# Ranking the instructions of two mixture-of-experts layers for the scheduler: routings and combinations at the start of the program, experts' blocks 200 places back, the rest as traced

## The chip, the core and the metric

The kernel runs on one core of a Trainium2 chip. Its engines work beside each other, each through its own list of instructions: TensorE (PE, with its weight loads as PEld), VectorE (DVE), ScalarE (ACT) and GpSimd (POOL); SyncE (SP) issues DMAs and computes nothing. GpSimd issues the indirect DMAs of this kernel. The metric is the device time of one execution in microseconds, the median of several runs.

## The reference, cut to what matters

Four layers work on `x` of 4 batches x 1024 tokens x 128 channels. Each is a "macaron": half a feed-forward block, an attention, the same half feed-forward again. All blocks take `layernorm(x)`, and all are added to `x`.

```python
x = x + 0.5 * _L0_ffn_ref(_layernorm(x, axis=-1), ...)   # mixture of 8 experts, gelu, the best 2 of a token
x = x + _L0_attn_ref(_layernorm(x, axis=-1), ...)        # per token: 16 heads against 16 heads
x = x + 0.5 * _L0_ffn_ref(_layernorm(x, axis=-1), ...)
x = x + 0.5 * _L1_ffn_ref(...)                           # gated feed-forward, silu
x = x + _L1_attn_ref(...)                                # full attention over 1024 tokens, rotary
x = x + 0.5 * _L1_ffn_ref(...)
x = x + 0.5 * _L2_ffn_ref(...)                           # mixture of 8 experts, relu, the best 2
x = x + _L2_attn_ref(...)                                # linear attention with decay
x = x + 0.5 * _L2_ffn_ref(...)
# layer 3: RWKV channel mix, time mix, channel mix
```

A mixture layer takes for each token the two experts with the largest router logits, runs each on it (128 to 512, an activation, back to 128), and adds the two results with softmax weights. Layers 0 and 2 are such layers, and the change concerns these alone.

## The kernel before, in words

`x` stays in SBUF as four tiles `x0` to `x3`, one for each batch, channels on partitions. The program has four stages: layer 0 with the first half feed-forward of layer 1; layer 1's attention (its matmuls ordered by hand); layer 2 with the second half feed-forward of layer 1 before it; layer 3.

In layers 0 and 2 the work is cut into tasks. A task is a Python generator: each `yield` ends a step and says what the step costs. The tasks of a pass n (0 ahead of the attention, 1 behind it) and a group of batches are:

- **route** (name `route{n}{first batch}`, line 284 on): normalised rows of the group go to memory (`rows`, line 307, a DMA on SP); logits; the best two of each token; a slot for each token and expert, so that every expert gets whole blocks of 128 slots; from that the index vectors `source` and `target` and the expert of each block. Most of it is a chain of small VectorE instructions. The last part sums 16 matmuls (a group of one batch) or 32 (two) into `held`, and the index vectors are made from it.
- **experts** (`experts{n}{first batch}`, line 421 on): one step a block, 23 blocks for a group of one batch and 39 for two. A block loads its expert's weights (`e_w`, 578 KB, line 455, a DMA on SP, 4 buffers), gathers 128 rows (`e_xg`, line 457, on POOL), transposes them on PE (line 461), copies (`e_x`, DVE), does four matmuls up, each followed by the activation on ACT (`e_h`, line 468), four matmuls down, an add (`e_y`, DVE, line 441) and a scatter to `res` (line 442, on POOL).
- **combine** (`combine{n}{batch}`, line 474 on): reads both results of each token back (`c_y`, line 487, two DMAs on SP, which wait for the group's scatters), weighs and adds them, transposes, and adds half to `x`.
- **middle** (`middle{batch}`): the layer's attention. In layer 0 it is VectorE's work: for each of 8 tiles of 128 tokens two products of 128x2048 (`prod`, lines 528 and 545), two reductions of them (lines 530 and 547), and small instructions. In layer 2 (lines 879 on) it is a recurrence over 8 tiles with some nine matmuls each.
- **last** (layer 0) and **first** (layer 2): layer 1's half feed-forwards.

The groups are (0), (1), (2, 3) in layer 0's first pass and (0, 1), (2), (3) in its second; in layer 2 (0, 1), (2, 3) in both. So layer 0 has 85 + 85 blocks and layer 2 has 78 + 78. A task starts in the trace when the tasks it names are done: experts after their route, combine after its experts, middle after its combine, route1 after the middles of its group.

`lanes` (line 1188) interleaves the tasks: each lane is a list of tasks in order, has a clock, and the lane with the least clock takes the next step and adds its cost. What comes out is only the order in which the instructions are traced. `macaron` (line 1208) makes the lanes: one of experts, one of combinations, and what `layer0` (line 1233) and `layer2` (line 1255) add (attention, feed-forward, routings).

After that a scheduler puts each engine's instructions in their final order. Each instruction has a rank, the value of a counter that goes up with each traced one; of those that could run next on an engine in its planning, the lowest rank goes first. This order is fixed in the program: an instruction that waits holds all behind it on its engine or queue. Before the change the rank is the place in the trace, so the lanes' interleaving decides.

Of the kernel before, what the change touches and what calls it, by code (L numbers as in the profile page):

```python
# [205 lines left out]
class Macaron:  # L206
# [981 lines left out]
    def lanes(self, *lanes):  # L1188
        lanes = [list(lane) for lane in lanes]
        clock, active, done = [0.0] * len(lanes), [None] * len(lanes), set()  # L1190
        while any(lanes) or any(active):
# [13 lines left out]
            else:  # L1205
                clock[n] += cost

    def macaron(self, name, moe, func, groups, marks, more):


        weights, (side, main), wp = self.packs[name + "m"], (self.side, self.main), self.fp
        plans = {}

        def plan(n, group):
            return plans.setdefault((n, group), {"mark": marks[n, group]})

        def route(n, group, *after, ps=side):
            return f"route{n}{group[0]}", after, lambda: self.route(ps, wp, moe, group, plan(n, group))

        def experts(n, group):  # L1220
            names = (f"route{n}{group[0]}",)
            return f"experts{n}{group[0]}", names, lambda: self.experts(main, wp, weights, func, group, plan(n, group))

        def combine(n, group):
            for b in group:
                yield f"combine{n}{b}", (f"experts{n}{group[0]}",), lambda b=b: self.combine(side, wp, group, b, plan(n, group))

        every = [(n, group) for n in range(2) for group in groups[n]]
        blocks = [experts(*g) for g in every]
        back = [task for g in every for task in combine(*g)]  # L1230
        self.lanes(blocks, back, *more(route))
# [140 lines left out]
```

## Time and profile before

| | us |
|---|---|
| median of 3 runs (3285.68 to 3298.78) | 3293.57 |
| the profiled execution | 3296.3 |
| its span, first to last instruction | 3294.4 |
| layer 0, with the loads ahead of it | 0 to about 942 |
| layer 1's attention | about 942 to 2037 |
| layer 2 | about 2037 to 2802 |
| layer 3 | about 2802 to 3294 |

| busy | us | share |
|---|---|---|
| PE | 2875.3 | 87% |
| PEld | 1685.8 | 51% |
| DVE | 1826.5 | 55% |
| ACT | 1649.2 | 50% |
| POOL | 807.0 | 24% |

The ends of some tasks in layer 0, from the instructions' times in the trace: experts00 start on PE at 49.4; experts01 end at 235; combine00 reads at 148.9 and middle0 starts at 160.8; experts02 run from 232 to 387; middle1 ends at 427.4; route10 runs from 430 to 515; experts10 from 515 to 670; middle3 ends at 729; experts13 end at 898. In layer 2: experts02 run from 2289 to 2451, the middles of batches 0 and 1 end at 2422, route10 at 2476; experts10 run from 2479 to 2647, the middles of 2 and 3 end at 2593, route12 runs from 2591 to 2650, experts12 from 2653 to 2781.

The page of the profile gives busy time of each engine, the granted clock of TensorE, the chain of work that ended last, and the costliest groups of instructions. A matmul's end is modelled, so a busy PE is not a PE at its peak. Idle time of an engine matters only where the chain goes through it.

### The profile page before, as it was taken

The page shows a single profiled execution, that of the slowest core. Times are in us where ns is not written, and L with a number is a line of the kernel's source. Part 1 is how long each engine was busy: PE and PEld are TensorE (multiplying, and loading weights), DVE is VectorE, ACT ScalarE, POOL GpSimd, SP SyncE. Part 2 cuts the span into 40 slices and gives each one's busy share as a digit, 9 for nine tenths or more (in the row PEclk, how much of TensorE's full clock was granted, in tenths as well). Part 3 has the DMA queues.
Part 4 walks back from the last instruction along what each step waited for, and adds up shares of the span by engine and source line. Part 5 has one row for each costly group of instructions (what it writes and reads, how often), then busy time and mean ns, then how long its engine had stood idle before and what let it go on. Part 6 is the DMA issues. An engine that isn't in the chain of part 4 may idle for free.

```text
span 3294.4 us, 48535 instructions
## 1 busy us (share of the span) xinstructions
PE 2875.3 (87%) x18206; PEld 1685.8 (51%) x18206; DVE 1826.5 (55%) x3160; ACT 1649.2 (50%) x3640; POOL 807.0 (24%) x748
## 2 busy tenths in 40 slices
PE   6888637878879999999999999988988977899997
PEld 6766426766643333333333333586777865344333
DVE  3376877774226676676776772431555521355664
ACT  3565524658613565566566565444444534444442
POOL 2565405552340000000000000046434454011110
PEclk7989858889977999999999999979989988788997
DMA  4766414663500000000000000157565666000000
GB/s 151 227 186 188 140 42 130 185 188 115 168 9 7 4 6 4 6 6 4 21 5 6 1 1 9 42 152 245 171 185 147 199 197 194 0 0 0 7 7 13
DMA packets 122890, 277.64 MB, mean 84 GB/s; under 512 B 18016, under 2 KB 67296, under 8 KB 122528
## 3 DMA queue, kind: packets, MB, share of 16 engines
q1 hardware_dynamic: 101792, 231.77, 23.8%
q0 software_dynamic: 20864, 42.77, 4.3%
q8 instruction: 144, 2.36, 0.3%
q14 instruction: 90, 0.74, 0.1%
HBM read 238.43 MB, written 31.85 MB: 82 GB/s over the span
## 4 chain that ended last, share of the span: by engine, by line
PE 74%; DVE 12%; ACT 5%; issue 4%; DMA 3%; POOL 1%; another core or an unknown queue 0%; SPq 0%; ACTq 0%; DVEq 0%; POOLq 0%
PE bank L227 40%; PE two L227 17%; PE o L227 8%; PE s L227 4%; DVE nm L720 2%; ACT e_h L468 2%; PE wave L1010 1%; DVE prod L545 1%; PE bank L461 1%; DMA c_y<-res 1%; DVE sc L530 1%; ACT L468 1%; DMA e_w<-in_l0m_dram 1%; DVE prod L528 1%; DVE e_x L463 1%
## 5 line engine op out<-in xcount | busy, mean ns | idle before, releaser
L720 DVE TENSOR_REDUCE nm<-two 128x2 f32<-128x1024 f32 x512 | 626.9, 1225 | 288.3 <-PE s L227 268.9
L743 ACT ACTIVATE e<-s 128x512 f32<-128x512 f32 x1024 | 556.4, 595 | 405.6 <-PE s L227 402.6
L468 ACT ACTIVATE e_h<-bank,e_w 128x128 f32<-128x128 f32 x1304 | 454.8, 368 | 511.6 <-PE bank L227 388.4
L227 PE MATMUL bank<-e_x,e_w 128*128 128x128 f32 x2608 | 569.3, 318 | 154.5 <-ACT e_h L468 79.9
L227 PE MATMUL s<-qm,kz 32*128 32x512 f32 x2048 | 634.1, 643 | 0.8 <-ACT e L743 0.8
L227 PE MATMUL two<-kz,qz 32*128 32x512 f32 x2048 | 593.2, 664 | 21.3 <-DVE nm L720 2.5
L227 PEld LDWEIGHTS bank<-e_x,e_w 128*128 128x128 f32 x2608 | 413.9, 204 | 291.3 <-ACT e_h L468 144.4
L457 POOL DMA_INDIRECT e_xg<-rows,g_source x326 | 334.4, 1026 | 835.1 <-DVE g_target L412 354.2
L227 PE MATMUL bank<-e_w,e_h 128*128 128x128 f32 x2608 | 445.7, 291 | 12.3 <-ACT e_h L468 6.9
L442 POOL DMA_INDIRECT res<-e_y,g_target x326 | 373.5, 1146 | 337.0 <-DVE e_y L441 152.7
L227 PEld LDWEIGHTS bank<-e_w,e_h 128*128 128x128 f32 x2608 | 378.8, 205 | 23.0 <-ACT e_h L468 13.3
L227 PE MATMUL o<-e,va 128*32 128x256 f32 x4096 | 328.8, 392 | 0.1
L441 DVE TENSOR_TENSOR e_y<-bank,e_w 128x128 f32<-128x128 f32 x326 | 94.3, 290 | 403.7 <-PE bank L227 317.0
L227 PEld LDWEIGHTS two<-kz,qz 32*128 32x128 f32 x2048 | 159.7, 189 | 239.9 <-issue 164.0
L227 PEld LDWEIGHTS o<-e,va 128*32 128x32 f32 x4096 | 81.0, 108 | 390.3 <-issue 370.3
L227 PEld LDWEIGHTS s<-qm,kz 32*128 32x128 f32 x2048 | 206.9, 183 | 10.9 <-issue 7.7
L708 POOL COPY va<-vd 128x256 f32<-128x256 f32 x16 | 6.7, 433 | 626.3 <-PE o L227 538.0
L1115 POOL TENSOR_TENSOR z<-st,r 128x512 f32<-128x512 f32 x32 | 46.2, 1445 | 417.1 <-DVE st L1108 333.7
L463 DVE COPY e_x<-bank 128x128 f32<-128x128 f32 x326 | 93.0, 285 | 92.2 <-PE bank L461 67.6
L227 PE MATMUL bank<-g_cols,g_lanes 128*128 128x39 f32 (+1 forms) x512 | 90.5, 341 | 28.9 <-DVE g_cols L392 28.8
L461 PE MATMUL bank<-c,e_xg 128*128 128x128 f32 x326 | 95.0, 291 | 21.7 <-DMA e_xg<-rows,g_source 21.6
L227 PEld LDWEIGHTS bank<-g_cols,g_lanes 128*128 128x128 f32 x512 | 91.2, 270 | 32.5 <-issue 31.4
(300 smaller groups left out, 3694.0 us busy)
## 6 DMA issues: line engine op xcount, KB each, us to landing
e_w<-in_l0m_dram SPq DMA_DIRECT2D x170, 578.0 KB
e_w<-in_l2m_dram SPq DMA_DIRECT2D x156, 578.0 KB
c_y<-res SPq DMA_DIRECT2D x32, 512.0 KB
rows<-g_xt SPq DMA_DIRECT2D x16, 512.0 KB
e_xg<-rows,g_source POOLq DMA_INDIRECT x326
res<-e_y,g_target POOLq DMA_INDIRECT x326
x<-in_x_dram SPq DMA_DIRECT2D x4, 512.0 KB
qz<-qd SPq DMA_DIRECT2D x64, 32.0 KB
```

The lines of the kernel that those rows point to most:

```text
L227: self.nc.tensor.matmul(out, lhsT, rhs, start=start, stop=stop)
L441: nc.vector.tensor_tensor(y, o, w[:, MOE_W - D :], ALU.add)
L442: ins = nc.gpsimd.indirect_dma_start(out=res[:, :], out_offset=at(target[:, k : k + 1]), in_=y, in_offset=None)
L457: nc.gpsimd.indirect_dma_start(out=xg, out_offset=None, in_=rows[:, :], in_offset=at(source[:, k : k + 1]))
L461: nc.tensor.transpose(tp, xg, self.c0["ident"])
L463: nc.vector.tensor_copy(x, tp)
L468: nc.scalar.activation(h[:, fc, :], up[:, fc, :], func, bias=w[:, 2 * FC * P + fc : 2 * FC * P + fc + 1])
L528: v.tensor_tensor(pr, q.unsqueeze(2).to_broadcast(sh), k.unsqueeze(1).to_broadcast(sh), ALU.mult)
L530: v.tensor_reduce(sc, pr, AX.X, ALU.add)
L720: v.tensor_reduce(nm[:, it, h, 2 * pair : 2 * pair + 2], s, AX.X, ALU.max, negate=True)
L743: nc.scalar.activation(es[g], s, AF.Exp, scale=scale)
L1115: (pool if i else v).tensor_tensor(z, st[:, 0:HALF], r, ALU.mult)
```

## The change

A new generator `ahead` runs each step of a task inside the scheduler library's context `high_priority(offset)`. With no offset the counter is set to 0, the start of the program, for the instructions of that step; with an offset it is set back by so much, and can fall below 0. At the end of the step the counter has its old value again, so instructions of such steps do not advance it. Routings and combinations are wrapped without an offset, experts with 200. Attention and feed-forward are not wrapped; they alone advance the counter, by some 130 for a middle of layer 0. What the tasks compute, their tiles and the lanes stay as they are.

```diff
+    def ahead(self, task, offset=None):
+
+        while True:
+            with self.tc.high_priority(offset=offset):
+                cost = next(task, None)
+            if cost is None:
+                return
+            yield cost
...
         def route(n, group, *after, ps=side):
-            return f"route{n}{group[0]}", after, lambda: self.route(ps, wp, moe, group, plan(n, group))
+            return f"route{n}{group[0]}", after, lambda: self.ahead(self.route(ps, wp, moe, group, plan(n, group)))
 
         def experts(n, group):
             names = (f"route{n}{group[0]}",)
-            return f"experts{n}{group[0]}", names, lambda: self.experts(main, wp, weights, func, group, plan(n, group))
+            return f"experts{n}{group[0]}", names, lambda: self.ahead(self.experts(main, wp, weights, func, group, plan(n, group)), 200)
 
         def combine(n, group):
             for b in group:
-                yield f"combine{n}{b}", (f"experts{n}{group[0]}",), lambda b=b: self.combine(side, wp, group, b, plan(n, group))
+                yield f"combine{n}{b}", (f"experts{n}{group[0]}",), lambda b=b: self.ahead(self.combine(side, wp, group, b, plan(n, group)))
```

## The prediction

> **What bounds the kernel now.** I read the chain that ended last first, to see which engine carries the end; then the busy times by stretch, to see where that engine stands idle; then the experts' blocks counted by stretch; then the chain inside two hand-overs.
>
> ```profile
> PE 74%; DVE 12%; ACT 5%; issue 4%; DMA 3%; POOL 1%; another core or an unknown queue 0%; SPq 0%; ACTq 0%; DVEq 0%; POOLq 0%
> ```
>
> TensorE carries 74% of the chain, but layers 0 and 2 are not dense on it (columns: stretch, length, busy us and count of PE, PEld, DVE, ACT, POOL, granted clock, DMA share, GB/s):
>
> ```profile
> 232.00:387.00 155.00, 121.49 (x738) 99.05 (x736) 119.07 (x182) 95.74 (x219) 93.26 (x75) 0.92 0.60 184
> 387.00:428.00 41.00, 10.67 (x26) 5.73 (x27) 35.03 (x46) 7.29 (x23) 0.94 (x1) 0.50 0.19 53
> 428.00:515.00 87.00, 41.42 (x166) 33.67 (x164) 62.51 (x96) 23.06 (x72) 1.96 (x2) 0.54 0.12 40
> ...
> 2420.00:2479.00 59.00, 45.17 (x300) 41.84 (x298) 27.98 (x88) 27.76 (x105) 15.11 (x16) 0.77 0.60 181
> 2479.00:2593.00 114.00, 108.32 (x742) 92.57 (x743) 69.94 (x215) 45.95 (x120) 52.81 (x54) 0.98 0.53 154
> 2593.00:2653.00 60.00, 51.22 (x364) 47.35 (x362) 25.57 (x87) 29.30 (x106) 26.80 (x26) 0.89 0.69 200
> ```
>
> From 387 to 515 us no experts run: first VectorE finishes the attention of batch 1 (middle1; VectorE 35.0 of 41 us), then the routing of the second pass (route10) waits on it. PE does 52 us of work in 128. That is layer 0's hole, and only the chain middle → route → experts can shorten it. In layer 2, middle, route and experts run side by side; the hole there is 26 us, and the chain shows it between the last routing step and the first gather:
>
> ```profile
> 2453.08 23.21 issue
> 2476.31 0.19 issue
> 2476.49 2.53 DMA e_xg<-rows,g_source
> ```
>
> The last routing, beside experts10 (2593 to 2653), leaves none: PE is busy 51 of 60 us. What experts alone can do is the last stretch (by tile e_y, one VectorE add per block):
>
> ```profile
> 515.00:670.00 155.00, 11.14 (x39) 52.09 (x38) 0.91 0.61 182
> 2653.00:2781.00 128.00, 11.37 (x39) 37.53 (x38) 0.94 0.72 217
> ```
>
> 39 blocks in 128 us, 3.3 us each; beside attention in layer 0 it is 4.0.
>
> **The Trainium skill.** "TensorE: Matmul & The Clock Gate", Step-by-step, says that matmuls stay in program order and only weight loads are pulled ahead; "Perfetto Trace Analysis", Tensor Engine Instruction, calls ACT, DVE and GpSimd strict FIFO. So the order in which the program is written is the order of execution, and a late instruction holds all behind it. The trace's records agree: they line up with the program's order on each engine. The first page (What's actually happening) lets the array fall to half clock after an idle window of about 3.4 us; the trace agrees, 0.50 and 0.54 in the two idle stretches. "ScalarE: Activation LUTs", What ACT_TABLE_LOAD costs, gives 1283 ns; the trace has 1283.
>
> **The change part by part.** No arithmetic, transfer or tile is added or removed; instructions move on all engines and on SP's and GpSimd's queues. I take places from the two built orders and durations from the trace. One thing is not as the words say: in layer 0 the counter stands at 28 when the experts start, so "200 ahead" is below zero, ahead of routings and combinations (which start at 0) until 200 attention instructions have passed. In layer 2 the counter is above 7300, and experts are only ahead of attention.
>
> *Layer 0.* (1) On PE the first experts' matmul goes from place 52 to 100, behind route01 and half of route02; on ACT 30 more instructions of 0.28 to 0.39 us stand before its first GELU: +10, start at 60. (2) experts00 and experts01 took 49 to 235 with route02 and middle0 among them. Now they stand almost alone: 23 blocks at 3.7 (cold start) and 23 at 3.35 give 85 + 77, end at 222, 13 earlier. (3) But combine00's two reads go from place 31 on SP to 53, behind all loads of experts01, and route02's second rows store from 24 to 55. After 222 come the read (6 us, as at 389.65 in the chain), the combination (5), 32 matmuls of route02 that now stand there (10), index vectors and the first gather (3): 24 us that were hidden. experts02 start at 246, was 232; middle0 starts some 70 us later than its 161. (4) experts02: 39 blocks at 3.6 beside middle0 alone, end 386, as before (385). But middle1's first VectorE instruction now stands at place 414 of VectorE's order, next to the last of experts02 (415), so 74 of its 75 are still to come when experts02 end, where 26 were left before. A middle is 8 tiles of two products (2.26), two reductions (2.28) and 1.8 us of small ones, and 1.4 for the residual: 88 us; combine02 and 03 stand inside with 8. So middle1 ends at about 484, was 427: **+57**, all without experts (48 more instructions at 1.18 us on average say the same). (5) From there route10, middle2 and the start of experts10 have the same places: shift unchanged. middle3's first PE place goes from 1202 to 1311, 109 matmuls of 0.3, less what experts10 gain: +28. It has then fewer experts among it (-10), and 441 instead of 504 matmuls are left after it (-18). Layer 0: **+57**.
>
> *Layer 2.* (6) experts02's last matmul goes from PE place 1177 to 1073, middle1's from 1057 to 1155, route10's first from 1060 to 1141. experts02 then need 39 x 3.4, to 2422; about half of both middles is left, four rounds of 7 us (9 beside experts in the trace), to 2450; route10 then runs with no experts to cover it. Its VectorE 20, ACT 11 and PE's part of 13 us are one chain, 45 us (58 beside experts, 2591 to 2650). experts10 start at 2495, was 2479: +16. (7) The same at the next hand-over, where there was no hole: experts10 end at 2626, middle3 27 later, route12 45 and the gather 3: 2701, was 2653: 48 in all. (8) combine10 moves into that hole, out of experts12's way: -5. experts00 start 51 places earlier, but route02's second store stands between weight loads on SP (place 23, was 10) and holds those behind it until batch 3 is normalised: I take the two as even. Layer 2: **+43**.
>
> Layers 1 and 3 keep their order (one swap). The table loads fall from 203 to 170, 33 x 1.283 = 42 us of ACT, which is idle half of the time: taken as nothing beyond the block times above; bounds 0 and -42, the latter if ACT paced the blocks. Bounds of the middle's tail in layer 2 (not seen alone in the trace): 20 to 36 for four rounds; of a routing alone, 32 (VectorE and GpSimd only) to 58.
>
> Sum against the profiled execution: 3296.3 + 57 + 43 = 3396; the median shown is 2.7 below that execution, so **3393**.
>
> **Rivals.** (a) *The attention chain of layer 0 has slack.* Against it: 387 to 515 has no experts and the chain runs through it. For it: experts10, 12 and 13 are spaced 4.0, 5.0 and 4.4 us and may catch up from 3.3. Then layer 0 gives nothing or a little and layer 2 its 43: 3335. (b) *Faster: the experts' stream sets the end.* Spacing above 3.3 us sums to about 150 us in layer 0 (19 + 16 + 25 + 26 + 39 + 25 over its six groups) and 71 in layer 2. Experts first could take this back; it decides once more than 100 of 221 come back without opening holes elsewhere. With 130 back: 3263. Against: the groups wait for routings, which wait for attention, which now comes last. (c) *Slower still:* middle3 keeps its +28, and SP stalls behind route02's store and combine03's second read, with PE at half clock in the new holes: +20 to +60, 3435. (d) *No effect:* excluded by the orders, unless holes and gains cancel: 3294.
>
> **How the numbers follow.** Forecast 0.52; (a) 0.24; (c) 0.11; (d) 0.05; (b) 0.08. Half a per cent, 16 us, is what a measurement of this kernel can tell from no change. Slower: 0.52 + 0.24 + 0.11 = 0.87; same 0.05; faster 0.08. The range leaves out (b), (d) and the far end of (c): 3318 to 3450. The forecast's own range, from the bounds of tail and routing and of the block times (3.3 to 3.7), is 3355 to 3430.
>
> **What would show it.** In layer 0, combine00 after experts01's last block (near 222) and experts02 some 20 us behind; middle0 starting near 230; a stretch of about 100 us with VectorE dense, the clock near 0.5 and no experts before route10; middle1 ending near 484. In layer 2, route10 and route12 starting after the experts before them have ended, with holes of 45 to 75 us in the e_y adds. Wrong if middle1 ends before 445, if experts10 and 12 of layer 0 come at 3.4 us beside attention, or if a routing alone takes under 30 us.

## The result, and the profile after

The changed kernel takes 3504.3 us (median of 4 runs, 3497.1 to 3508.9) against 3296.2 us of the kernel before on the same chip (4 runs, 3285.7 to 3302.4). The ratio is 1.065, interval 1.063 to 1.068: 208 us slower. The forecast was 3393, +99 us; the direction was right, the size half of what came, and outside the range.

The profiled execution took 3497.1 us (span 3495.1), 200.8 more than the one before. By stage, from the instructions' times in the trace:

| | before | after | difference | forecast |
|---|---|---|---|---|
| layer 0, end | 942 | 1048 | +106 | +57 |
| layer 1's attention, length | 1095 | 1095 | 0 | 0 |
| layer 2, length | 765 | 858 | +93 | +43 |
| layer 3, length | 493 | 494 | +1 | 0 |

The loss is where the change is, and in both layers about twice what I had. First the shares of the span on the chain that ended last, after:

```profile
PE 57%; DVE 7%; DMA 2%; ACT 2%; issue 2%; POOL 1%; another core or an unknown queue 0%; SPq 0%; ACTq 0%; DVEq 0%; POOLq 0%
```

The shares sum to 71%, not 100: this chain can be followed back only to 1006 us, so it shows nothing of layer 0 but its last 42 us, and PE's 57% against 74% before is no comparison (57 of 71 is 80%). Layer 0 has to be read from the stretches (after; columns: stretch, length, busy us and count of PE, PEld, DVE, ACT, POOL, granted clock, DMA share, GB/s):

```profile
78.00:160.00 82.00, 65.29 (x412) 57.11 (x412) 25.74 (x89) 38.37 (x108) 50.46 (x51) 0.89 0.68 200
160.00:227.00 67.00, 54.14 (x375) 46.01 (x375) 12.49 (x44) 29.90 (x88) 37.66 (x39) 1.00 0.83 243
227.00:262.00 35.00, 25.84 (x98) 21.75 (x99) 10.64 (x29) 8.41 (x21) 6.21 (x7) 0.50 0.37 105
262.00:408.00 146.00, 121.33 (x718) 101.05 (x717) 103.12 (x155) 88.54 (x203) 84.64 (x72) 0.88 0.57 175
408.00:503.00 95.00, 18.73 (x43) 9.11 (x42) 89.34 (x95) 15.57 (x41) 2.77 (x1) 0.53 0.08 23
503.00:590.00 87.00, 40.58 (x167) 32.74 (x165) 61.86 (x95) 23.08 (x72) 1.79 (x2) 0.54 0.12 40
590.00:741.00 151.00, 119.67 (x739) 100.07 (x739) 81.14 (x155) 87.67 (x219) 87.05 (x77) 0.90 0.57 174
741.00:770.00 29.00, 10.74 (x40) 8.70 (x40) 24.06 (x49) 8.21 (x22) 3.78 (x5) 0.51 0.46 145
862.00:900.00 38.00, 32.70 (x126) 18.76 (x126) 22.97 (x73) 17.01 (x41) 2.95 (x5) 0.87 0.34 110
```

The first two rows are experts00 and experts01, almost alone (VectorE 26 and 12 us busy), the best stretch at full clock and 243 GB/s. What follows gives it back. From 227 to 262 combine00 and route02 run with no experts, at half clock. From 262 to 408 experts02 run beside middle0 alone. The row of 408 to 503 is middle1: VectorE 89 of 95 us, PE 19 at a clock of 0.53. The same stretch, from the end of experts02 to route10, was 41 us before. Route10 (503 to 590) is what it was. Two further holes are new: 741 to 770, between experts10 and experts12, and 862 to 900, between experts12 and experts13 (38 us, was 11).

Layer 2 after, same columns:

```profile
2391.00:2532.00 141.00, 122.74 (x854) 106.32 (x853) 54.38 (x177) 66.41 (x188) 71.91 (x73) 0.99 0.67 209
2532.00:2578.00 46.00, 31.45 (x172) 25.38 (x172) 28.67 (x90) 9.23 (x32) 0.97 (x1) 0.89 0.13 36
2578.00:2623.00 45.00, 24.90 (x117) 22.48 (x117) 23.37 (x68) 9.81 (x40) 2.35 (x3) 0.54 0.27 90
2623.00:2764.00 141.00, 125.92 (x855) 108.82 (x855) 51.88 (x166) 61.44 (x171) 73.48 (x75) 0.95 0.58 183
2764.00:2806.00 42.00, 29.35 (x145) 25.16 (x146) 24.50 (x78) 8.79 (x32) 0.97 (x1) 0.81 0.15 40
2806.00:2853.00 47.00, 27.13 (x118) 24.50 (x116) 23.17 (x70) 9.50 (x39) 3.00 (x3) 0.50 0.25 87
2853.00:2980.00 127.00, 103.04 (x664) 89.90 (x662) 23.30 (x79) 53.47 (x156) 72.19 (x74) 0.91 0.68 203
```

Row by row: experts02; the rest of the two middles with no experts; route10 alone; experts10; the rest of the other two middles; route12 alone; experts12. The rows of experts02 and experts10 are 141 us where they were 162 and 168, but the four rows between experts sum to 180 us, where the holes before were 28 and 7. The blocks counted by their adds (tile e_y; after), to compare with the two lines of before:

```profile
590.00:741.00 151.00, 10.94 (x39) 0.90 0.57 174
2853.00:2980.00 127.00, 11.28 (x39) 0.91 0.68 203
```

39 blocks in 151 and 127 us, 155 and 128 before: where the same work stands beside the experts, their pace is the same.

The chain inside the tail of the middles, after, shows why that tail is long (start us, length, what):

```profile
2547.47 0.33 DVE kv L894
...
2548.45 1.17 PE bank L227 x8
2549.64 0.30 DVE den L917
...
2549.97 0.95 DVE den L918
...
2551.42 0.33 DVE kv L894
```

Each 128-token tile is a chain of 3.95 us (2547.47 to 2551.42): 1.17 us of matmuls, the rest small VectorE instructions one behind the other, the reciprocal of line 918 the longest. The next tile's first VectorE instruction comes when this tile's last but one is done. The tiles of the two batches do not overlap, so a round of one tile of each costs 7.9 us.

And the hand-over from routing to experts in layer 2, in the chain of after:

```profile
2618.77 0.21 DVE g_source L409
...
2620.04 2.57 DMA e_xg<-rows,g_source
```

There is no slack between index vectors and gather: experts10 wait for the routing itself. That is not new. Before, too, the gather followed its index vectors at once (timeline of before; start us, length, engine, line, operation, in brackets the idle time and what ended it):

```profile
2471.40 3.63 PE L227 MATMUL bank<-g_cols,g_lanes 128*128 128x39 f32 x16
2475.52 0.20 DVE L409 SCALAR_TENSOR_TENSOR g_source<-g_w,g_far 128x39 uint32<-128x39 f32 x1
2476.49 0.98 POOL L457 DMA_INDIRECT e_xg<-rows,g_source  x1 [23.41 <-issue]
```

The prediction read the 23 us of "issue" in that chain as a hole behind the last routing step. The routing runs inside it: its position matmuls go on to 2475.0. What is new after the change is that a whole routing runs with no experts beside it, not only its last 26 us.

### The profile page after: what moved, and what is told of

It reads as the page before. It is cut to its first block, busy times and chain, and to the rows that moved or that the text cites. A ratio compares the mean times of both kernels' runs of the same rounds, so it can differ in the third digit from the quotient of the medians.

```text
span 3495.1 us, 48681 instructions
## 1 busy us (share of the span) xinstructions
PE 2938.3 (84%) x18206; PEld 1737.5 (50%) x18206; DVE 1840.6 (53%) x3160; ACT 1602.5 (46%) x3607; POOL 780.2 (22%) x748
## 4 chain that ended last, share of the span: by engine, by line
PE 57%; DVE 7%; DMA 2%; ACT 2%; issue 2%; POOL 1%; another core or an unknown queue 0%; SPq 0%; ACTq 0%; DVEq 0%; POOLq 0%
PE bank L227 26%; PE two L227 16%; PE o L227 8%; PE s L227 4%; DVE nm L720 2%; PE wave L1010 1%; DMA e_w<-in_l2m_dram 1%; DMA c_y<-res 1%; PE bank L461 1%; DVE st L1108 1%; PE acc L1010 1%; DVE kv L1101 1%; PE bank L1010 1%; DVE den L918 0%; ACT e_h L468 0%
## 5 line engine op out<-in xcount | busy, mean ns | idle before, releaser
L468 ACT ACTIVATE e_h<-bank,e_w 128x128 f32<-128x128 f32 x1304 | 446.3, 367 | 561.0 <-PE bank L227 467.6
L227 PE MATMUL bank<-e_x,e_w 128*128 128x128 f32 x2608 | 552.0, 318 | 149.3 <-ACT e_h L468 74.3
L457 POOL DMA_INDIRECT e_xg<-rows,g_source x326 | 339.5, 1041 | 1063.7 <-DVE g_target L412 365.4
L227 PE MATMUL bank<-e_w,e_h 128*128 128x128 f32 x2608 | 466.5, 293 | 9.8 <-ACT e_h L468 5.8
L442 POOL DMA_INDIRECT res<-e_y,g_target x326 | 341.7, 1048 | 336.9 <-DVE e_y L441 227.7
L227 PEld LDWEIGHTS bank<-e_w,e_h 128*128 128x128 f32 x2608 | 393.5, 206 | 20.6 <-ACT e_h L468 12.5
L227 PE MATMUL bank<-g_cols,g_lanes 128*128 128x39 f32 (+1 forms) x512 | 100.2, 369 | 55.0 <-DVE g_cols L392 55.0
L227 PEld LDWEIGHTS bank<-g_cols,g_lanes 128*128 128x128 f32 x512 | 101.6, 299 | 62.6 <-issue 48.9
```

Of the source, the lines that this page charges most:

```text
L227: self.nc.tensor.matmul(out, lhsT, rhs, start=start, stop=stop)
L442: ins = nc.gpsimd.indirect_dma_start(out=res[:, :], out_offset=at(target[:, k : k + 1]), in_=y, in_offset=None)
L457: nc.gpsimd.indirect_dma_start(out=xg, out_offset=None, in_=rows[:, :], in_offset=at(source[:, k : k + 1]))
L468: nc.scalar.activation(h[:, fc, :], up[:, fc, :], func, bias=w[:, 2 * FC * P + fc : 2 * FC * P + fc + 1])
```

## The experiments

Every time is set against runs of the kernel before on the same chip. The runs fell on other chips than the first comparison (medians of the kernel before 3213, 3214 and 3284 us there, 3296 on the first), so ratios are compared, and microseconds of a stage only within a chip's pace. The chips with 3213 and 3214 us count as one pace below.

### The two kernels again

A copy of each, to have stage lengths on the chip of the other runs.

> The kernel before, unchanged, for its trace on the chip of this call. The chip of the runs so far gave 3213 us where the first gave 3296. If the chips differ in the pace of the transfers, layers 0 and 2 (1707 us together before) are the shorter ones, by about 80 us, and layers 1 and 3 the same within 5 us; if they differ in the clock of TensorE, layers 1 and 3 are shorter as well.

> The changed kernel, unchanged, for its trace and ratio beside the kernel before on this chip. Theory A (holes ahead of the routings and attention that runs alone; none of it is transfer time): the loss is about 200 us here too, ratio 1.06 to 1.07. If faster transfers make the experts' stream denser and attention the bound earlier, the loss is larger: 1.075 to 1.09.

The copy of the kernel before took 3209.6 us (one run; the median of nine on that chip is 3214.4), the changed kernel 3399.6, ratio 1.058, 1.055 to 1.061. Layer 0 ends at 904 and 1002 (+98), layer 2 is 714 and 805 long (+91). The loss is of the same kind on a chip where the whole is 2 to 3% faster. In the kernel before, layer 0 is 38 us and layer 2 51 us shorter than on the first chip, while layers 1 and 3, which load no experts' weights, are as long as there.

### The experts' part of the change alone

```diff
-            return ..., lambda: self.ahead(self.route(...))
+            return ..., lambda: self.route(...)
...
-                yield ..., lambda b=b: self.ahead(self.combine(...))
+                yield ..., lambda b=b: self.combine(...)
```

> Only the experts are ranked 200 places back; routings and combinations keep their place in the trace. Theory A (the experts' lead is the whole loss: attention ends behind the experts, and the next routing then has no experts beside it): middle1 of layer 0 still has 74 of 75 VectorE instructions after experts02, and the middles of layer 2 still have 55 and 28 of 158 left after experts02 and experts10 (79 and 69 in the changed kernel), so layer 0 stays near +80 to +105 and layer 2 near +60 to +85: 3435 to 3485 us. Route00's rows store is first on SP's queue again, so the experts start near 50 and not 78. Theory B (routings and combinations at the start of the program are what hurts, by standing in the queues ahead of work that is ready): at most +50, 3296 to 3345 us.

3340.0 us, ratio 1.040, 1.037 to 1.042. Layer 0 ends at 967 (+63), layer 2 is 787 long (+73). Putting the experts 200 places ahead is by itself most of the loss, though layer 0 lost less than theory A said.

### Routings and combinations alone

```diff
-            return ..., lambda: self.ahead(self.experts(...), 200)
+            return ..., lambda: self.experts(...)
```

> Only routings and combinations are ranked at the start of the program; the experts keep their place in the trace. Theory A: no loss, 3270 to 3305 us; in layer 2 route10 stands at PE places 1054 to 1188 (before 1060 to 1217), so the hole ahead of experts10 (26 us before) shrinks by up to 15 us. Theory B: most of the loss of the changed kernel is here, 3400 us or more.

3291.5 us, ratio 1.024, 1.022 to 1.027. Layer 0 ends at 957 (+53), layer 2 is 746 long (+32). That is neither theory: A had no loss, B most of it. The hole ahead of experts10 in layer 2 closes, and the layer gets longer. What happened is in the stretches of route10 beside experts02 in layer 2 (this run; columns as above):

```profile
2460.00:2465.00 5.00, 4.43 (x23) 4.46 (x24) 2.01 (x4) 0.56 (x2) 1.27 (x1) 0.60 0.46 141
2465.00:2470.00 5.00, 5.00 (x26) 5.00 (x25) 1.39 (x2) 0.45 (x2) 0.00 (x0) 0.50 0.00 0
2470.00:2475.00 5.00, 5.00 (x25) 5.00 (x25) 1.78 (x4) 0.66 (x2) 0.22 (x1) 0.50 0.00 0
```

PE is busy and the clock is at half, while no byte moves for 10 us: this is the routing's position step, 32 matmuls from g_cols and g_lanes (64 records in the trace, two for each). By the order of the trace they run from 2460.6 to 2477.6 with 10 of the experts' matmuls between them, so activation, scatter, gather and weight loads stand still behind them. In the kernel before, this step of layer 2's route02 has 56 of the experts' matmuls between its 32, and that of route12 has 21. The group of these matmuls shows the price (line, operation, shapes, count, busy us, mean ns, idle before); first the copy of the kernel before, then this run:

```profile
L227 PE MATMUL bank<-g_cols,g_lanes 128*128 128x39 f32 x384 | 60.9, 321 | 24.0 <-DVE g_cols L392 23.8
```

```profile
L227 PE MATMUL bank<-g_cols,g_lanes 128*128 128x39 f32 x384 | 74.4, 370 | 20.1 <-DVE g_cols L392 20.1
```

Ranked first, a routing runs as a lump wherever it stands. It is not hidden by being beside the experts, because on each in-order engine the experts are behind it.

### Combinations alone

```diff
-            return ..., lambda: self.ahead(self.route(...))
+            return ..., lambda: self.route(...)
...
-            return ..., lambda: self.ahead(self.experts(...), 200)
+            return ..., lambda: self.experts(...)
```

> Only the combinations are ranked at the start of the program. Their places move by some tens at most (combine00 stays at SP places 31 and 32). If combinations were what cost routings and combinations together 2.4%: ratio 1.015 to 1.025. If it was the routings: 0.997 to 1.003.

3219.0 us, ratio 1.002, 1.000 to 1.005: nothing that can be told from no change. What the run before this one lost is the routings'.

### The routings of the second pass alone

```diff
-            return ..., lambda: self.ahead(self.route(...))
+            return ..., lambda: self.ahead(self.route(...)) if n else self.route(...)
```

with experts and combinations as traced.

> Only the routings of the second pass (route10, route12 and, in layer 0, route13) take rank 0; all else is as traced. The routings-first run lost 53 us in layer 0 and 32 in layer 2 and shows a routing's position step (matmuls from g_cols and g_lanes) in one lump, with 10 matmuls of the experts between its 32 (before: 56 and 21 for the two that ran beside experts). Theory 'lump': a routing ranked first runs as if alone wherever it stands, and the experts' stream stretches by what it would have taken alone. Layer 2's hole of 29 us between experts02 and experts10 closes, but experts02 and experts10 grow by as much or more: layer 2 +5 to +15, layer 0 +5 to +10 (route10 is alone there in any case), ratio 1.003 to 1.008. Rival 'hole': the closed hole is gained, and the routings-first run lost its time with the first pass's routings: layer 2 20 to 25 us shorter, ratio 0.993. Either way the first pass's part of that run's loss is what this leaves out.

3302.2 us against 3284.2, ratio 1.005, 1.003 to 1.007: "lump" holds, "hole" does not. The two stretches of layer 2 with experts and a routing side by side (this run):

```profile
2300.00:2488.00 188.00, 173.31 (x1131) 149.87 (x1129) 99.47 (x315) 81.38 (x245) 79.01 (x80) 0.92 0.57 171
2482.00:2673.00 191.00, 171.97 (x1120) 149.96 (x1120) 96.72 (x313) 78.78 (x242) 81.64 (x83) 0.92 0.56 168
```

experts02 take 188 us and experts10 192. There is no hole between them: experts10 start 7 us before experts02 have ended. The attention run with 100 places, further down, has layer 2 in the order of before on the same chip: there they take 161 and 164, with holes of 28 and 7. So 45 us of holes were closed (28 + 7 and 7 + 3), and the two groups grew by 27 and 28. With experts02 starting 12 us later and experts12 5 us shorter, layer 2 is 770 us long against 752. By its size this is the whole loss of the run; in layer 0, which ends at 945, the second pass's routings changed little, so most of the +53 of the routings-first run comes from the first pass's.

### Ranks kept above zero

```diff
     def macaron(self, name, moe, func, groups, marks, more):
+        self.tc.cur_priority += 1000
```

The counter starts each of the two layers 1000 higher, so that in layer 0 too the experts stay behind routings and combinations and ahead of the rest. In layer 2 nothing changes by it.

> As the changed kernel, but the counter is raised by 1000 ahead of each of the two layers, so that 200 places back never falls below the rank of routings and combinations. Theory A with the below-zero part of it (in layer 0 the experts stood ahead of combine00 and of the stores of rows): combine00 returns to SP place 32, middle0 to PE place 396, middle1 has 48 of 75 left after experts02 instead of 74, and the experts start near 55 instead of 78: layer 0 is +50 to +75 instead of +106, layer 2 unchanged at +93: 3440 to 3465 us. If being below zero does not matter: 3490 to 3510 us.

3369.2 us, ratio 1.049, 1.047 to 1.051. Layer 0 ends at 973 where the changed kernel ends at 1002; layer 2 is 805 in both. So ranks below zero cost 30 us, and the other 69 of layer 0 do not depend on them. combine00 starts on PE at 167 (changed kernel 218, before 139), middle0 at 184 (225, 145), middle1 ends at 451 (479, 410).

### Experts 20 places ahead instead of 200

```diff
+        self.tc.cur_priority += 1000
...
-            ..., lambda: self.ahead(self.experts(...), 200)
+            ..., lambda: self.ahead(self.experts(...), 20)
```

> As the kernel with the raised counter, but the experts 20 places ahead instead of 200, about one block. Theory A: the loss grows with the lead; in layer 2 nothing of the middles is left after the experts (79 and 69 instructions with 200), and middle1 of layer 0 has 39 left (48 with 200, 26 before). What remains is what routings and combinations alone cost, 1.024, and a few us: ratio 1.025 to 1.035. If the lead's size does not matter: 1.045 to 1.05.

3304.3 us, ratio 1.029, 1.028 to 1.031. Against the run before this one only the distance differs: layer 2 falls from 805 to 731, layer 0 from 973 to 970. Layer 2's hand-over with 200 places (run with the counter high: middles' tail, route10 alone), and with 20 (experts02, hand-over, experts10):

```profile
2440.00:2484.00 44.00, 29.49 (x163) 23.73 (x162) 26.61 (x84) 8.48 (x28) 0.86 (x1) 0.90 0.14 38
2484.00:2530.00 46.00, 26.23 (x121) 23.51 (x120) 24.90 (x71) 10.41 (x44) 2.04 (x2) 0.54 0.26 88
```

```profile
2307.00:2484.00 177.00, 161.09 (x1129) 140.84 (x1128) 97.72 (x314) 81.37 (x245) 74.69 (x76) 0.99 0.60 185
2484.00:2488.00 4.00, 0.02 (x1) 0.02 (x1) 0.00 (x0) 0.00 (x0) 3.09 (x4) 0.51 0.72 214
2488.00:2670.00 182.00, 168.55 (x1118) 149.07 (x1118) 97.94 (x314) 80.38 (x243) 80.93 (x83) 0.93 0.56 170
```

With 20 places no instruction of a middle is left behind the experts, and 90 us of hand-over become 4; the second hand-over, 86 us, closes as well. The experts pay for it with 177 and 182 us instead of 136 and 129. The difference of the two kernels in layer 2 is the hand-overs less what the experts pay, as theory A had it. In layer 0 the distance makes no difference: middle1 ends at 448 with 20 places and at 451 with 200.

### The store of rows first on the sync queue

The changed kernel's first gather waits for a store, as its queues show (start us, length, queue, line, operation; in brackets the idle time and what ended it):

```profile
69.70 1.01 SPq L307 DMA_DIRECT2D rows<-g_xt  x2
```

```profile
75.00 1.14 POOL L457 DMA_INDIRECT e_xg<-rows,g_source  x1 [74.11 <-DMA rows<-g_xt]
```

The index vectors of route00 were there at 56.3. Its store of rows stands on SP behind one of route02, which waits for rows that are normalised later. I took this 20 us for a part of what I had missed. The test gives route00 of layer 0 the lowest rank of all:

```diff
-            ..., lambda: self.ahead(self.route(...))
+            ..., lambda: self.ahead(self.route(...), 1000 if <route00 of layer 0> else None)
```

> The changed kernel, but the first routing of layer 0 (route00) is ranked 1000 ahead, below the experts' ranks, so that its store of rows is written on the sync queue before the first-pass store of route02, which waits for batches 2 and 3. Theory 'store order': the first gather waited for that store and nothing else; the experts of layer 0 then start at 50 to 56 us instead of 78, the whole stream of layer 0 shifts with them, and layer 0 ends 20 to 28 us sooner than the changed kernel's 1002: ratio 1.050 against its 1.058. Rival 'absorbed': experts01 and the side's attention end where they did, since the first blocks wait for other work (the second routing, the weights' stream), layer 0 gains under 8 us, ratio 1.056 or more.

3494.9 us against 3284.2, ratio 1.064, 1.060 to 1.068; the changed kernel had 1.065 and 1.058. "Absorbed" holds. PE at the start of layer 0 in this run:

```profile
49.44 0.47 PE L461 MATMUL bank<-c,e_xg 128*128 128x128 f32 x1 [1.74 <-DMA e_xg<-rows,g_source]
54.27 0.59 PE L227 MATMUL bank<-g_cols,g_lanes 128*128 128x23 f32 x2 [4.36 <-DVE g_cols L392]
...
68.06 0.63 PE L227 MATMUL bank<-e_x,e_w 128*128 128x128 f32 x2
```

The gather comes 28 us sooner and the first block is transposed at 49.4. Its matmuls then stand behind route01's position step and route02's transposes until 68.1, and of the gathers seven go out, then the eighth waits for PE until 69.2, since there are six buffers. experts01 end at 221 (changed kernel on the first chip, of nearly the same pace: 226), middle1 at 499 (503), layer 0 at 1041 (1048), and the ratio is that of the first chip. The store was late, and hardly anything hung on it.

### Attention first, and attention a little ahead

Three runs try the opposite of the change. In the first, the middles of both layers take rank 0 with routings and combinations, experts as traced:

```diff
-            attn = lambda b, *after: (..., lambda: self.l0_attn(side, pa, m, b))
+            attn = lambda b, *after: (..., lambda: self.ahead(self.l0_attn(side, pa, m, b)))
...
-            attn = lambda b: (..., lambda: self.l2_attn(...))
+            attn = lambda b: (..., lambda: self.ahead(self.l2_attn(...)))
```

> The reverse of the change: routings, combinations and the attention (middles) of layers 0 and 2 at the start of the program, the experts and the feed-forwards as traced behind them. Theory A (the chain middle, routing, next experts sets the end, and experts are the work that fills): middle1 of layer 0 has 13 of 75 left after experts02 (26 before), middle3 ends at PE place 1550 (1613), route10 of layer 2 ends at PE place 1044, 163 ahead of experts10, so the 26 us hole in layer 2 closes: 3225 to 3275 us. Theory C (the experts' own pace sets the end, whoever is first): experts slowed by 2.3 us VectorE instructions ahead of their copies, 3300 to 3350 us.

3455.3 us, ratio 1.077, 1.074 to 1.079: worse than the change itself, and against what I expected. Layer 0 ends at 1090, layer 2 is 775 long. In layer 2 no hole is left between experts02 and experts10. In layer 0, experts02 take 206 us (286 to 492) instead of 152 in the copy, and middle1 still ends 34 us behind them:

```profile
286.00:492.00 206.00, 125.79 (x734) 99.06 (x732) 116.14 (x173) 84.91 (x208) 76.88 (x73) 0.79 0.44 137
```

PE's work in the row is near that of experts02 in the copy (126 us, there 118 in 152), and neither PE nor VectorE is dense. So the other two runs move only layer 0's attention, all else as in the kernel before, by 100 and 300 places:

```diff
-            attn = lambda b, *after: (..., lambda: self.l0_attn(side, pa, m, b))
+            attn = lambda b, *after: (..., lambda: self.ahead(self.l0_attn(side, pa, m, b), 100))
```

> Kernel before, but layer 0's attention of all four batches is ranked 100 ahead; routings, experts and combinations as traced. By places, 13 of middle1's 75 VectorE instructions come behind the last experts02 instruction (before: 26), and 16 of middle3's behind experts10 (before: 32). Theory 'path': in layer 0 the chain middle1, route10, experts10 sets the end, so what is moved ahead of the experts is gained: middle1 ends 10 to 18 us sooner, middle3's part is a few us more; ratio 0.993 to 0.997. Rival 'lump', as with attention first: the attention's chains stand in front of the experts' steps in the queues, experts01 and experts02 grow by as much as the tail shrinks: ratio 0.999 to 1.005.

> As the run before it with 300 places instead of 100: 13 of middle1's 75 and 13 of middle3's come behind the experts, and middle0 starts before combine00 has ended by places. Theory 'path': a little more than with 100, ratio 0.992 to 0.996. Rival 'lump': more of the attention in one piece between the experts, experts01 and experts02 grow by 15 us or more, ratio 1.005 to 1.02.

3315.0 us, ratio 1.009, 1.006 to 1.011, and 3361.6 us, ratio 1.025, 1.021 to 1.029. Both miss "path" and go the way of "lump", by more than its ranges. The run with the second routings alone has this part in the order of before and ran on the same chip: there experts01 end at 231, experts02 at 382 and middle1 at 422. With 100 places it is 245, 408 and 442, with 300 places 259, 438 and 472. The tail of middle1 behind the experts is 34 us in both instead of 41, but all ahead of it is later by 26 and 56 us. With 300 places it then takes 124 us instead of 88 from there to experts10; VectorE is busy for 101 of the 124, for 62 of the 88. No version that was tried is faster than the kernel before.

## Why the prediction was half right

The direction and the path were right, and two terms failed. In layer 0 it is step 5, the shift that was to stay as it was behind middle1: it grew by 31 of the 49 us that were missing. In layer 2 it is the size of the middles' tail: 33 of the 50 us.

**The order of the signs.** That middle1 runs alone after experts02, that layer 2's hand-overs open, and that neither is paid back, came as forecast. The rivals "attention has slack", "faster" and "no effect" fall with the rows of 408 to 503 and 2532 to 2623. Rival (c), slower still, was nearest in sum. One of its terms came true, middle3's (step 5); another did not: the run with route00's store first on SP shows that at the start of layer 0 the queue behind route02's store was not it. Its third, combine03's second read, did go out late (473.6 us, before 399.6), but no experts ran until 590; no run takes it apart.

**Layer 0, +57 forecast, +106 measured.**

*Step 1*, experts start at 60, was 78. The term I left out is SP's order: I counted places on PE and ACT and not that route00's store had moved behind route02's. It carried only 4 us on, experts01 ending at 226 instead of the 222 of *step 2*, since the two groups then took 148 us where I had 162. Two errors nearly cancel, and that is luck; the run with the store first shows that the start did not decide the end.

*Step 3*, the hand-over after experts01, was sized 24 us and took 36 (226 to 262). Read and combination took the 11 us I had. The 32 matmuls I had at 10 us, hidden pace; in a lump at half clock they took 15.8 (237.4 to 253.3). From there to the experts' first transpose I had 3 us and it took 8.9: the gather goes out at 254.7, but middle0's first matmuls stand ahead of the transpose on PE.

*Step 4*: experts02 took 146 us where I had 140, and middle1 alone 95 where I had 98. It ends at 503 instead of 484, and the 19 us are 4 of step 2, 12 of step 3 and 6 of experts02, less 3 of its own. The mechanism, attention that begins late and ends behind the experts, is what the trace shows and the runs agree with. On one pace of chip, middle0 starts at 145, 182, 184, 194 and 225 us in the kernel before, with 20 places, with the counter high, with experts alone and in the change; middle1 ends at 410, 448, 451, 448 and 479; layer 0 ends at 904, 970, 973, 967 and 1002. A first combination that comes some 40 or 80 us later goes with a layer 0 some 65 or 100 us longer. Among the three in the middle the order is not kept (the latest start has the earliest end), so the start is not all of it.

*Step 5*, "shift unchanged", is the one that failed. I let middle3's +28 be paid back by experts10 (-10) and by the fewer matmuls after it (-18). From the trace of after, against before: the shift is 75 where experts10 start; experts10 give 5 back; the new hole to experts12 costs 31 (experts12 started 3 us before experts10's end, now 28 behind); experts12 give 24 back; the hole to experts13 costs 27; the rest about 2. Sum 106. The gains do exist, and the openings they were to pay are twice their size. In the first hole route12 stands half done: its choice of experts is ready at 701.8 us, but its next matmul starts only at 737.5, behind experts10's on PE, and the rest of it shares VectorE with middle3. In the second, route13 follows middle3, which ends at 845 (before 729). In the terms of step 5, middle3 starts 40 us later than the shift explains, where I had 28, and from its end to experts13 the way is 12 us shorter, where I had 28. Rival (c) had named this ("middle3 keeps its +28").

**Layer 2, +43 forecast, +93 measured.** By row, lengths of the stage's pieces on the first chip:

| step | forecast | measured | what was mis-sized |
|---|---|---|---|
| up to experts02's start | 0 | -5 | experts00 start 25 us sooner and take 23 longer |
| 6, experts02 | 133 us | 141 | +8: 3.4 us a block taken, 3.6 measured |
| 6, hand-over | 73 | 91 | +18: tail 46, not 28; route10 alone 45, as forecast |
| 7, experts10 | 131 | 141 | +10, as in step 6 |
| 7, hand-over | 75 | 89 | +14: tail 42, not 27; route12 alone and gather 47, 48 forecast |
| 8, combine10 out of experts12 | -5 | 0 | +5 |

The misses sum to +50, and 43 and 50 make the 93. Here the mechanism was right, and the term that failed is a size, wrong twice: the tail of the middles, 46 and 42 us for 28 and 27. I took "four rounds of 7 us" from the 9 us of a round beside experts. Alone, a round is 7.9 us, as the chain above shows. In the first tail four rounds were left, but ahead of them stand 11.7 us, to 2543.7: the end of a tile and the second half's normalisation and projections of one batch. They are in no term of mine. The last tile ends 3 us late, behind route10's first matmuls. In the second tail the four rounds themselves took 39.5 us (2766.4 to 2805.9). My bounds for the tail, 20 to 36, left out 42 and 46. That the lead is what costs is shown by the run with 20 places: no tail is left, the routings run beside the experts, and layer 2 is 74 us shorter.

**Table loads.** 33 fewer (203 to 170) taken as nothing: nothing in the runs contradicts it, and none isolates it; in layer 0 experts10's pace beside attention is nearly the same, 151 us for 39 blocks against 155.

**The addition.** I had added the changes of order as if routings first were free where they stand beside experts. The runs price the two parts apart: routings and combinations first +53 and +32, experts ahead +63 and +73, both +98 and +91 on the same pace of chip. They do not add up. A likely reason, which no run shows, is that a routing that runs alone in a hole cannot hold experts up as well.

**What stays open.** Why attention ahead by 100 or 300 places makes experts01 and experts02 of layer 0 slower, where its tail becomes shorter by places, is read from the stretches and only argued: on in-order engines the experts' small VectorE steps stand behind long attention instructions. No run took these apart. The part of the first pass's routings in layer 0 (about +45 of +53) is a difference of two runs on different chips, not a run of its own; it fits that the routings-first run is already 29 us behind the copy when experts01 end (249 against 220). Why middle3 of layer 0 starts 40 us later than the shift was not tested either.

## What to carry to other kernels

A rank for a scheduler that fixes in-order queues is not a priority on the chip: in these runs what was ranked first was written as one piece, and what shared an engine with it stood behind. Before ranking a stream ahead, count what is left behind its last instruction on the engine of the next link (here VectorE of the attention), price that remainder as a chain alone, and let every routing that follows it run alone too, at the clock of such a stretch (0.54 and 0.50 here). A hole in the busiest engine is not a gain to be had: here closing 45 us of holes lengthened the experts around them by 55.

## What the runs showed that I had not expected

- Two chips differed in the pace of the mixture layers alone: the same program took 904 and 942 us to the end of layer 0 and 714 and 765 us in layer 2, with layers 1 and 3 equal, 2.6% of the whole. The runs do not show why.
- The 32 position matmuls of layer 2's route02 and route12 keep PE busy for 7.9 and 8.1 us in the copy of before, with 56 and 21 of the experts' matmuls between them and a clock of 1.00, and for 12.5 and 12.6 us with routings first, at 0.57 and 0.55. In route10 of that run the clock is 0.51 over 17.1 us in which PE is recorded as busy throughout; such a lump did not bring the clock up. One piece is not always slow: route00 of layer 2 runs there at 1.00 and takes 7.6 us of PE.
- A store that held the first gather for some 20 us was worth at most some 5 us at the end of the experts behind it.
